# A recurrent layer with a feed-forward gate: order of the first projections, of z and of the odd products

## The chip, the cores and the metric

The kernel runs on one core of a Trainium2 chip. The metric is the device time of one execution in microseconds (us), as the median of several runs. The engines are called PE (TensorE, matrix products), DVE (VectorE), ACT (ScalarE), POOL (GpSimd) and SP (SyncE); each works through its own queue of instructions, and SP and POOL also issue the DMA transfers here.

## The reference

All in float32, S = 2048 tokens, hidden width 512, H = 16 heads of D = 128, four lags:

```python
xn = layernorm(x)                                    # 2048 x 512
q, k, v = (conv4(silu(xn @ W)) for W in (Wq, Wk, Wv))  # causal, 4 taps per channel, 2048 x 2048
z, a, b = xn @ Wz, xn @ Wa, xn @ Wb                  # a, b: 16 wide
q, k = rotary(q), rotary(k)                          # then each head divided by its norm
out = 0
for s in range(4):                                   # lag s: s tokens earlier
    attn = einsum('bshd,bshd->bsh', q, lag(k, s)) / sqrt(D)
    out += (attn * sigmoid(lag(a, s) * b))[..., None] * lag(v, s)
out = out * rsqrt(mean(out * out) + eps) * norm_w * silu(z)
s = out @ Wout                                       # 2048 x 512
hidden = relu((xn @ sign(up).T) * up_scale)          # 2048 x 2048
g = silu((hidden @ sign(down).T) * down_scale * out_scale)
return x + s * g
```

## The kernel before

**Tiling.** Features lie on the 128 partitions and tokens along the free axis. The tokens are cut into NTB = 4 blocks of TB = 512 (index b), the 16 heads into NP = 8 pairs (index p); a pair has two halves j of 128 channels. `xnT` holds the normalised input feature-major. One projection of a pair (pq, pk, pv or pz) is 8 matmuls of 128x512 with K = 4 chunks, each seen as two rows of the profile, so sixteen rows.

**A step.** `step(p, b)` first makes `queries(p, b + 1)` and `products(p, b + 1)`: pq, silu, a convolution by one ACT multiply and three DVE operations for each half; pk in the same way; the rotation by lags (`turn`); and the products of q and k for four lags, tile `pr`, first for half 0 and then for half 1. For blocks after the first and odd p, half 1 goes through the tile `half` in two parts (L367 to L370); for even p it fills a second `pr` tile and a POOL DMA adds it. The sums over channels (`dots`) are made by PE from pairs of p. Then, for block b itself: pv, the convolution of v (`values`), the output projections that are due (`output_projections`, with `sum_dots` in the middle), the load of the z weights, the load of `wo`, pz (`gates_of_output`), the weighted sum over lags (`weighted`: `o` from `v` and the coefficients `bc`, seven DVE operations), and `gated_output` (`oz`: two DVE operations). After an odd p, the output projection of the pair p - 1, p is put on a list; it is worked off in the next step. So the projection of pairs 0 and 1 is done in step p = 2, and that of 2 and 3 in step p = 4. The gated output of p = 0 is held back until step p = 1 (`first_due`).

**Around the blocks.** A first pass of steps with b = -1 makes the q and k side of block 0, with the feed-forward part of block 0 between. Three passes follow, and then the last block has a loop of its own (L756), which only has v, z and the output side. The coefficients of a block are written to DRAM (`co_dram`) and loaded again as `bc`, spread over the partitions. At the end come the feed-forward products of blocks 1 to 3 and the gate of the outputs.

**What sets the order.** What goes through the class `InOrder` (`pe`, `dve`, `pool`, and `loads["by"]` in the last block) stays in the program's order on its engine; all of it shows as L76 in the profile. What is issued by `nc.scalar`, `nc.sync` and `nc.gpsimd` directly is placed by a scheduler within the dependencies. The tile q has one buffer, `pr` two, the weights' tile `w` three, the PSUM pool `mm` six banks.

**The start.** Four chunks of x are loaded, measured, normalised (`first_layer_norm`) and transposed on PE (`transpose`), each followed by an idle matmul that keeps PE busy (`idle_work`). Only then comes the first pq.

Of the kernel before, what the change touches and what calls it, by code (L numbers as in the profile page):

```python
# [44 lines left out]
P = 128  # L45
# [4 lines left out]
LAGS = 4  # L50
# [31 lines left out]
def recurrent_layer(ctx: ExitStack, tc: tile.TileContext, a: dict, out: bass.AP):  # L82
    nc = tc.nc
    pe, dve = InOrder(tc, nc.tensor), InOrder(tc, nc.vector)

    pool = InOrder(tc, nc.gpsimd)
    loads = {"by": nc.sync}

    const = ctx.enter_context(tc.tile_pool(name="const", bufs=1))
# [42 lines left out]
    nc.gpsimd.memset(no_ab, 0.0)  # L132

    def small_loads():
        nc.sync.dma_start(conv_w, a["conv_w"])
        nc.sync.dma_start(w_ab, a["w_ab"])
        nc.sync.dma_start(ab_dram[:, 0:HALO], no_ab)
        nc.sync.dma_start(turns, a["turns"])
        nc.sync.dma_start(of_head, a["of_head"])
        nc.sync.dma_start(of_heads, a["of_heads"])  # L140
        nc.sync.dma_start(norm_w, a["norm_w"])
        nc.sync.dma_start(up_scale, a["up_scale"])
# [3 lines left out]

    def first_layer_norm():

        mv = qks.tile([P, TC, 2], F32, tag="mv", name="mv0", bufs=2)
        rstd = qks.tile([P, TC], F32, tag="rstd", name="rstd0", bufs=2)  # L150
        x_in = qks.tile([P, TC, HID], F32, tag="pr", name="x_in0", bufs=2)

        def normalise(c):
            one = slice(c, c + 1)
            nc.scalar.activation(rstd[:, one], mv[:, one, 1], AF.Sqrt, bias=eps_ln)
            dve.reciprocal(rstd[:, one], rstd[:, one])
            dve.tensor_scalar(
                x_in[:, c, :], x_in[:, c, :], mv[:, c, 0:1], rstd[:, one], ALU.subtract, ALU.mult
            )

        for c in range(TC):
            nc.sync.dma_start(x_in[:, c, :], a["x"][c * P : (c + 1) * P, :])
            st = qks.tile([P, 6], F32, tag="st", name=f"st{c}", bufs=2)
            dve.bn_stats(st, x_in[:, c, :])
            dve.bn_aggr(mv[:, c, :], st)
            if c:
                normalise(c - 1)
        normalise(TC - 1)
        return x_in

    def transpose(x_in, idle_work):
        for c in range(TC):
            tp = mm.tile([P, KC, P], F32, tag="mm", name=f"tp{c}")
            for k in range(KC):
                pe.transpose(tp[:, k, :], x_in[:, c, k * P : (k + 1) * P], ident)
            idle_work(TB // 2)
            nc.scalar.copy(xnT[:, :, HALO + c * P : HALO + (c + 1) * P], tp)  # L177

    means = {}

    def statistics(b, c):
# [79 lines left out]
    def keep_halo(name, t, p, b):  # L261
        if b < NTB - 1:
            nc.scalar.copy(kept[name][:, p], t[:, :, TB : TB + HALO])

    def project(n, p, b, to):
        for j in range(2):
            pp = mm.tile([P, TB], F32, tag="mm", name=f"p{n}{j}_{p}_{b}")
            for k in range(KC):
                pe.matmul(
                    pp,  # L270
                    weights[n][:, k, j * P : (j + 1) * P],
                    xnT[:, k, HALO + b * TB : HALO + (b + 1) * TB],
                    start=(k == 0),
                    stop=(k == KC - 1),
                )
            nc.scalar.activation(to[:, j, :], pp, AF.Silu)
# [27 lines left out]

    def queries(p, b):

        load(qks, "q", p, b)
        q = qks.tile([P, LAGS, 2, TB], F32, tag="q", name=f"q_{p}_{b}", bufs=1)
        q0 = q[:, LAGS - 1]
        convolve(0, p, raw_of(qks, "q", p, b), q0)  # L310
        return q
# [16 lines left out]
    def products(p, b, q, between=None, beside_k=None):  # L328

        n = f"_{p}_{b}"  # L330
        load(qks, "k", p, b)
        q0 = q[:, LAGS - 1]
        k = with_halo(qks, "k", "k", 1, p, b)
        raw = raw_of(qks, "k", p, b)
# [24 lines left out]
        if not b or p % 2 == 0:  # L359
            pr1 = qks.tile([P, LAGS, TB], F32, tag="pr", name="pr1" + n, bufs=2)  # L360
            product(pr1, 1, 0, LAGS)
            if b:
                nc.gpsimd.dma_start(pr, pr1, accum_op=ALU.add)
            elif p < NP - 1:
                dve.tensor_tensor(pr, pr, pr1, ALU.add)
        else:
            for lo in range(0, LAGS, 2):  # L367
                half = qks.tile([P, 2, TB], F32, tag="half", name=f"half{lo}" + n, bufs=1)
                product(half, 1, lo, lo + 2)
                dve.tensor_tensor(pr[:, lo : lo + 2], pr[:, lo : lo + 2], half, ALU.add)  # L370
        if not b:

            prs = [pr, pr1] if p == NP - 1 else [pr]
# [191 lines left out]
    def step(p, b, beside_q=None, beside_k=None):  # L565

        at = b >= 0
        change = p == 0 and at
        q = queries(p, b + 1)
        if beside_q:  # L570
            beside_q()
        if change and b:
            sum_squares()
            norms(b)
        due = bool(dots_due) and dots_due[0][-1]
        if change and not b:

            def beside_k():
                norms(b)
                norms_in_rows(b)  # L580

        products(p, b + 1, q, (lambda: norms_in_rows(b)) if change and b else None, beside_k)
        if p == NP - 1 and b + 2 < NTB:
            gate_products(b + 2)
        if at:
            load(vs, "v", p, b)
            raw = raw_of(vs, "v", p, b, 1)
        if first_due:
            first_due.pop()()
        if at:  # L590
            v = values(p, b, raw)

        output_projections(sum_dots if due else None)
        if change:
            coefficients(b)
        if at:
            load(vs, "z", p, b)
            wo = load_wo(p, b)
            z = gates_of_output(p, b)
            out_of = lambda: gated_output(p, b, weighted(p, b, v), z, wo)  # L600
            if change:
                first_due.append(out_of)
            else:
                out_of()
        if p == 1 and at:
            gate(b + 1)
        if b + 2 < NTB:
            if p < TC:
                statistics(b + 2, p)
            if p == TC - 1:  # L610
                centre(b + 2)
            elif p == 5:
                divide(b + 2)
# [8 lines left out]

    for n in (TB, TB, TB // 2):
        idle_work(n)
    x_in = first_layer_norm()
    small_loads()
    transpose(x_in, idle_work)
    def in_two_terms(pool, x, tag, bufs, shape, name):
        hi = pool.tile(shape, F32R, tag=f"{tag}_hi", name=f"{name}_hi", bufs=bufs)
        lo = pool.tile(shape, F32R, tag=f"{tag}_lo", name=f"{name}_lo", bufs=bufs)  # L630
# [23 lines left out]
    with tc.tile_pool(name="pre", bufs=1, side="right") as pre:  # L654
        signs = {}

        def fetch(g, which):

            for f in range(G * g, G * g + G):
                raw = pre.tile([P, HID], F32, tag="raw", name=f"pre_{which}_raw{f}", bufs=4)  # L660
                src = a[which][f]
                nc.sync.dma_start(raw, src.rearrange("p k m -> p (k m)") if which == "up" else src)
                sign = pre.tile([P, HID], F32R, tag="sign", name=f"pre_{which}{f}", bufs=8)
                nc.scalar.activation(sign, raw, AF.Sign)
                nc.gpsimd.dma_start(signs_dram[which][:, f], sign)
                signs[which, f] = sign

# [25 lines left out]
                else:  # L693
                    nc.gpsimd.dma_start(to, part, accum_op=ALU.add)

        xs = in_two_terms(pre, tokens(0), "xs", 1, [P, KC, TB], "xs0")
        for p in range(NP):
            g = p // 2
            if p == 0:

                def first_ups():
                    fetch(0, "up")
                    ups(0, G)

                step(p, -1, None, first_ups)
            elif p % 2 == 0:
                step(p, -1, lambda: ups(G * g, G * g + 2), lambda: ups(G * g + 2, G * g + G))
            else:
# [22 lines left out]
    raw = raw_of(vs, "v", 1, last, 1)  # L731
    load(vs, "v", 2, last)
    wo = load_wo(0, last)
    sum_dots()
    coefficients(last)
    output_projections()
# [19 lines left out]
    for p in range(NP + 1):  # L756
        if 1 < p < NP:
            weights["v"] = v_weights.pop(p)
            raw = raw_of(vs, "v", p, last, 1)
        if p:  # L760
            z = gates_of_output(p - 1, last)
        if p % 2 == 1:
            output_projections()
        if 0 < p < NP:
            load(vs, "z", p, last)
            v = values(p, last, raw)
        if p and p + 2 < NP:
            load(vs, "v", p + 2, last)
# [27 lines left out]
    with tc.tile_pool(name="ff", bufs=1, side="right") as ff, tc.tile_pool(  # L796
# [6 lines left out]
        def ends(b, banks=None):  # L803
# [17 lines left out]
                    g, banks[c] if banks else g, out_scale, down_scale, ALU.mult, ALU.mult  # L821
                )

            def gate(c):
                rows, x, y, g = loaded[c]
                t = b * TC + c
                nc.scalar.activation(g, g, AF.Silu)
                dve.scalar_tensor_tensor(g, y, rms[:, t : t + 1], g, ALU.mult, ALU.mult)
                dve.tensor_tensor(g, g, x, ALU.add)
                nc.sync.dma_start(out[rows, :], g)  # L830

            return scale, gate

        def down_projection(c, f, terms):
# [10 lines left out]
        for b in range(1, NTB):  # L845
            pf = [pfs.tile([P, HID], F32, name=f"pf{c}") for c in range(TC)]
            for f in range(2, NFC + 2):
# [22 lines left out]
            scale, gate = ends(b, pf)  # L870
            if b == last:

                for cs in (0, 1), (2,), (3,):
                    for _, df, terms in hids:
                        for c in cs:
                            down_projection(c, df, terms)
                    for c in cs:
                        scale(c)
                        if c:
                            gate(c - 1)  # L880
                gate(TC - 1)
            else:

                for c in range(TC):
                    scale(c)

# [69 lines left out]
```

## Time and profile before

| what | value |
|---|---|
| median of 3 runs | 1429.37 us (1429.17 to 1430.85) |
| the profiled execution | 1430.83 us, its span 1429.0 us |
| mean granted clock of PE | 0.995 |
| busy: PE, DVE, ACT, POOL | 1405.1, 1209.7, 612.0, 231.3 us |
| chain that ended last | PE 63%, DVE 22%, issue 6%, DMA 3%, ACT 3% |

A group's row gives line, engine and operation, output and inputs, count, then busy time and mean ns of one, then the idle time of the engine ahead of it and what ended most of it. A row of the timeline gives start and duration in us, engine, line, operation, output and inputs, count, and in brackets the idle time before it with what ended that.

### The profile page before, as it was taken

What the parts mean: (1) busy time and instruction counts of PE and PEld (TensorE: products, weight loads), DVE (VectorE), ACT (ScalarE), POOL (GpSimd) and SP (SyncE); (2) the same over time, 40 slices, a digit from 0 to 9 for tenths busy, and PEclk for the clock granted to TensorE, in tenths of its full rate; (3) what the DMA queues carried; (4) which work ended last, traced back from release to release, by engine and by line L of the source; (5) the groups of instructions that cost most, each with busy time, mean ns of one, the idle gap of its engine ahead of it and who ended that gap; (6) DMA issues with size and microseconds to landing.
All of it is one profiled execution on the core that took longest, in us unless ns stands there. A gap on an engine that the chain in (4) does not pass through costs nothing.

```text
span 1429.0 us, 12596 instructions
## 1 busy us (share of the span) xinstructions
PE 1405.1 (98%) x3958; PEld 686.0 (48%) x3958; DVE 1209.7 (85%) x1363; ACT 612.0 (43%) x1181; POOL 231.3 (16%) x317
## 2 busy tenths in 40 slices
PE   9999999899999999999999999999999999999998
PEld 5555544344444444444444444444443444578886
DVE  6999988999999979999999899999995979146454
ACT  7475545445444443444434444444342323232122
POOL 2222121111212220112122201121211111200000
PEclk9999999999999999999999999999999999999999
DMA  9879676987998688779986897796848888662030
GB/s 327 252 195 206 154 200 133 250 194 190 188 226 194 135 176 234 201 166 196 220 205 147 168 236 192 177 206 174 165 88 211 238 208 203 125 235 90 30 89 30
DMA packets 101779, 259.22 MB, mean 181 GB/s; under 512 B 18833, under 2 KB 19345, under 8 KB 97361
## 3 DMA queue, kind: packets, MB, share of 16 engines
q0 software_dynamic: 33088, 104.89, 38.8%
q1 hardware_dynamic: 68624, 153.53, 35.4%
q8 instruction: 32, 0.52, 0.2%
q14 instruction: 35, 0.28, 0.1%
HBM read 157.67 MB, written 35.68 MB: 135 GB/s over the span
## 4 chain that ended last, share of the span: by engine, by line
PE 63%; DVE 22%; issue 6%; DMA 3%; ACT 3%; SPq 1%; POOL 0%; DVEq 0%; POOLq 0%; ACTq 0%
PE po L76 13%; PE pz L76 11%; PE pv L76 9%; PE pq L76 8%; PE pk L76 8%; PE pf L76 6%; PE ph L76 6%; DVE q L76 5%; DVE pr L76 3%; DVE k L76 3%; DVE o L76 3%; DVE te L76 2%; DVE v L76 2%; DVE half L76 1%; PE dots L76 1%
## 5 line engine op out<-in xcount | busy, mean ns | idle before, releaser
L76 PE MATMUL po<-wo,oz 128*128 128x512 f32 x512 | 228.8, 601 | 10.0 <-DVE oz L76 10.0
L76 PE MATMUL pz<-xnT,wz 128*128 128x512 f32 x512 | 227.2, 596 | 3.2 <-DMA wz<-in_wz_dram 3.2
L76 PE MATMUL pv<-xnT,wv 128*128 128x512 f32 x512 | 226.4, 594 | 0.0
L76 PE MATMUL pq<-xnT,wq 128*128 128x512 f32 x512 | 226.0, 593 | 0.2 <-ACT xnT L177 0.2
L76 PE MATMUL pk<-xnT,wk 128*128 128x512 f32 x512 | 225.2, 592 | 0.0
L76 PEld LDWEIGHTS po<-wo,oz 128*128 128x128 f32 x512 | 97.0, 192 | 139.1 <-issue 112.5
L76 DVE SCALAR_TENSOR_TENSOR k<-rk,conv_w,k 128x512 f32<-128x512 f32 x192 | 142.0, 751 | 25.4 <-ACT k L288 20.8
L76 DVE SCALAR_TENSOR_TENSOR q<-rq,conv_w,q 128x512 f32<-128x512 f32 x192 | 141.3, 749 | 22.1 <-ACT q L288 17.5
L76 PEld LDWEIGHTS pz<-xnT,wz 128*128 128x128 f32 x512 | 97.0, 190 | 129.1 <-issue 125.5
L76 PEld LDWEIGHTS pv<-xnT,wv 128*128 128x128 f32 x512 | 95.7, 189 | 127.7 <-issue 117.2
L76 PEld LDWEIGHTS pq<-xnT,wq 128*128 128x128 f32 x512 | 96.0, 189 | 126.1 <-issue 118.0
L76 PEld LDWEIGHTS pk<-xnT,wk 128*128 128x128 f32 x512 | 96.6, 189 | 121.0 <-issue 117.1
L76 DVE SCALAR_TENSOR_TENSOR v<-rv,conv_w,v 128x512 f32<-128x512 f32 x192 | 141.3, 750 | 4.8 <-ACT v L288 0.3
L76 DVE SCALAR_TENSOR_TENSOR q<-q,turns 128x1024 f32<-128x1024 f32 (+1 forms) x128 | 127.1, 1013 | 2.3
L76 DVE TENSOR_TENSOR o<-o,te 128x1024 f32<-128x1024 f32 x96 | 117.5, 1224 | 3.3
L76 DVE TENSOR_TENSOR pr<-q,k 128x2048 f32<-128x2048 f32 x52 | 117.3, 2286 | 0.9
L76 DVE TENSOR_TENSOR te<-v,bc 128x1024 f32<-128x1024 f32 x96 | 116.9, 1218 | 1.0 <-DMA bc<-co_dram 1.0
L649 ACT ACTIVATE hid<-ph,up_scale 128x512 f32<-128x512 f32 x64 | 43.8, 685 | 119.4 <-PE ph L76 118.8
L76 DVE CAST hid_hi<-hid 128x512 fp32r<-128x512 f32 x64 | 27.1, 423 | 71.9 <-ACT hid L649 71.9
L76 PE MATMUL ph<-xs_hi,up 128*128 128x512 f32 x192 | 76.4, 398 | 0.7 <-ACT so_sb L423 0.7
L76 PE MATMUL ph<-xs_lo,up 128*128 128x512 f32 x192 | 75.8, 395 | 0.0
L547 ACT COPY part<-po 128x512 f32<-128x512 f32 x64 | 37.1, 580 | 84.8 <-PE po L76 49.5
(142 smaller groups left out, 1662.6 us busy)
## 6 DMA issues: line engine op xcount, KB each, us to landing
bc<-co_dram SPq DMA_DIRECT2D x128, 256.0 KB, 6.4
pr<-pr POOLq DMA_DIRECT2D x72, 256.0 KB, 5.6
wq<-in_wq_dram SPq DMA_DIRECT2D x32, 512.0 KB, 6.5
wk<-in_wk_dram SPq DMA_DIRECT2D x32, 512.0 KB, 5.8
sq<-sq POOLq DMA_DIRECT2D x32, 512.0 KB, 5.7
wv<-in_wv_dram SPq DMA_DIRECT2D x32, 512.0 KB, 6.6
wz<-in_wz_dram SPq DMA_DIRECT2D x32, 512.0 KB, 6.0
wo<-in_wo_dram SPq DMA_DIRECT2D x32, 512.0 KB, 6.4
```

Source lines behind the costliest of these rows:

```text
L76: return self.tc.keep_in_program_order(getattr(self.engine, op)(*args, **kwargs))
L547: nc.scalar.copy(part, po)
L649: nc.scalar.activation(hid, ph, AF.Relu, scale=up_scale[:, f : f + 1])
```

## The change

Five edits:

- At the start, statistics and normalising go by halves of the four chunks, ACT keeps the program's order there (`act`), the loads of the first q and k weights go ahead of the small loads, and the first pq is computed by halves of the tokens (`first_product`): the first 256 tokens of both j after two chunks are transposed. Chunks 2 and 3 are transposed within it, and two idle matmuls are gone.
- In step p = 2 of each block, pz goes ahead of the output projections.
- For odd p after the first block, the product of half 1 is written into q's place (`q[:, :, 1]`) and then added to `pr`: for p = 1 by a POOL DMA of 1 MB, for the others by one DVE operation.
- In the last block the z weights of pairs 1 and on are requested one step sooner, those of pair 1 ahead of the coefficients.
- The last down projections of the feed-forward part go in another order of chunks, and the last operations of the ends are written out in one order.

```diff
+    act = InOrder(tc, nc.scalar)
...
     def small_loads():
-        nc.sync.dma_start(conv_w, a["conv_w"])
...
-        for c in range(TC):
-            nc.sync.dma_start(x_in[:, c, :], a["x"][c * P : (c + 1) * P, :])
...
-            if c:
-                normalise(c - 1)
-        normalise(TC - 1)
-        return x_in
...
+        for c in range(TC):
+            nc.sync.dma_start(x_in[:, c, :], a["x"][c * P : (c + 1) * P, :])
+        for half in range(2):
+            for c in range(2 * half, 2 * half + 2):
+                measure(c)
+            for c in range(2 * half, 2 * half + 2):
+                normalise(c)
+        transpose(0)
+        idle_work(TB // 2)
+        transpose(1)
+        idle_work(TB // 2)
+
+        return lambda: (transpose(2), transpose(3))
...
+    def first_product(to, second_half):
+
+        pps = [mm.tile([P, TB], F32, tag="mm", name=f"pq{j}_0_0") for j in range(2)]
+        for lo in range(0, TB, TB // 2):
+            for j in range(2):
+                for k in range(KC):
+                    pe.matmul(
+                        pps[j][:, lo : lo + TB // 2],
+                        weights["q"][:, k, j * P : (j + 1) * P],
+                        xnT[:, k, HALO + lo : HALO + lo + TB // 2],
+                        start=(k == 0),
+                        stop=(k == KC - 1),
+                    )
+                if lo == j == 0:
+                    second_half()
+        for j in range(2):
+            act.activation(to[:, j, :], pps[j], AF.Silu)
...
         else:
-            for lo in range(0, LAGS, 2):
-                half = qks.tile([P, 2, TB], F32, tag="half", name=f"half{lo}" + n, bufs=1)
-                product(half, 1, lo, lo + 2)
-                dve.tensor_tensor(pr[:, lo : lo + 2], pr[:, lo : lo + 2], half, ALU.add)
+
+            product(q[:, :, 1], 1, 0, LAGS)
+            if p == 1:
+
+                nc.gpsimd.dma_start(pr, q[:, :, 1], accum_op=ALU.add)
+            else:
+                dve.tensor_tensor(pr, pr, q[:, :, 1], ALU.add)
...
-        output_projections(sum_dots if due else None)
+        midway = sum_dots if due else None
+
+        late = at and p == 2
+        if not late:
+            output_projections(midway)
         if change:
             coefficients(b)
         if at:
             load(vs, "z", p, b)
             wo = load_wo(p, b)
             z = gates_of_output(p, b)
+            if late:
+                output_projections(midway)
...
-    x_in = first_layer_norm()
+    other_chunks = first_layer_norm()
+    load(qks, "q", 0, 0)
+    nc.sync.dma_start(conv_w, a["conv_w"])
+    load(qks, "k", 0, 0)
     small_loads()
-    transpose(x_in, idle_work)
...
     wo = load_wo(0, last)
+    z_weights = {0: weights["z"]}
+    load(vs, "z", 1, last)
+    z_weights[1] = weights["z"]
     sum_dots()
     coefficients(last)
...
         if p:
+            weights["z"] = z_weights.pop(p - 1)
             z = gates_of_output(p - 1, last)
         if p % 2 == 1:
             output_projections()
+        if 1 < p < NP:
+            load(vs, "z", p, last)
+            z_weights[p] = weights["z"]
         if 0 < p < NP:
-            load(vs, "z", p, last)
             v = values(p, last, raw)
...
-                for cs in (0, 1), (2,), (3,):
-                    for _, df, terms in hids:
-                        for c in cs:
-                            down_projection(c, df, terms)
-                    for c in cs:
-                        scale(c)
-                        if c:
-                            gate(c - 1)
-                gate(TC - 1)
+                downs(0, 0, n - 1)
+                downs(1, 0, 2)
+                downs(0, n - 1, n)
+                downs(1, 2, n)
+                by_y(0)
+                plus_x(0)
+                by_y(1)
+                downs(2, 0, n)
+                plus_x(1)
+                by_y(2)
+                downs(3, 0, n)
+                plus_x(2)
+                by_y(3)
+                plus_x(3)
```

Here `downs(c, lo, hi)` makes the products of chunk c with the hidden chunks lo to hi and, after the last of them, the chunk's scale and silu; `by_y` multiplies by the attention's output, `plus_x` adds x and stores the chunk.

More of the change, by code (lines that the diff above doesn't have):

```diff
@@ L151, in first_layer_norm, with measure @@
         x_in = qks.tile([P, TC, HID], F32, tag="pr", name="x_in0", bufs=2)
+        def measure(c):
+            st = qks.tile([P, 6], F32, tag="st", name=f"st{c}", bufs=2)
+            dve.bn_stats(st, x_in[:, c, :])
+            dve.bn_aggr(mv[:, c, :], st)
+            one = slice(c, c + 1)
+            act.activation(rstd[:, one], mv[:, one, 1], AF.Sqrt, bias=eps_ln)
         def normalise(c):
             one = slice(c, c + 1)
-            nc.scalar.activation(rstd[:, one], mv[:, one, 1], AF.Sqrt, bias=eps_ln)
             dve.reciprocal(rstd[:, one], rstd[:, one])
@@ L159, in normalise, with transpose @@
             )
-        for c in range(TC):
-            nc.sync.dma_start(x_in[:, c, :], a["x"][c * P : (c + 1) * P, :])
-            st = qks.tile([P, 6], F32, tag="st", name=f"st{c}", bufs=2)
-            dve.bn_stats(st, x_in[:, c, :])
-            dve.bn_aggr(mv[:, c, :], st)
-            if c:
-                normalise(c - 1)
-        normalise(TC - 1)
-        return x_in
-    def transpose(x_in, idle_work):
-        for c in range(TC):
+        def transpose(c):
             tp = mm.tile([P, KC, P], F32, tag="mm", name=f"tp{c}")
@@ L175, in transpose @@
                 pe.transpose(tp[:, k, :], x_in[:, c, k * P : (k + 1) * P], ident)
-            idle_work(TB // 2)
-            nc.scalar.copy(xnT[:, :, HALO + c * P : HALO + (c + 1) * P], tp)
+            act.copy(xnT[:, :, HALO + c * P : HALO + (c + 1) * P], tp)
+        for c in range(TC):
[10 more added lines that the diff above has]
+        return lambda: (transpose(2), transpose(3))
+    means = {}
     means = {}
@@ L263, in keep_halo @@
             nc.scalar.copy(kept[name][:, p], t[:, :, TB : TB + HALO])
+    def first_product(to, second_half):
[14 more added lines that the diff above has]
+            act.activation(to[:, j, :], pps[j], AF.Silu)
     def project(n, p, b, to):
+        if n == "q" and p == b == 0:
+            first_product(to, second_half)
+            return
         for j in range(2):
@@ L305, in queries @@
     def queries(p, b):
-        load(qks, "q", p, b)
+        if p or b:
+            load(qks, "q", p, b)
         q = qks.tile([P, LAGS, 2, TB], F32, tag="q", name=f"q_{p}_{b}", bufs=1)
@@ L330, in products @@
         n = f"_{p}_{b}"
-        load(qks, "k", p, b)
+        if p or b:
+            load(qks, "k", p, b)
         q0 = q[:, LAGS - 1]
@@ L663, in fetch @@
                 sign = pre.tile([P, HID], F32R, tag="sign", name=f"pre_{which}{f}", bufs=8)
-                nc.scalar.activation(sign, raw, AF.Sign)
+                (act if f < G else nc.scalar).activation(sign, raw, AF.Sign)
                 nc.gpsimd.dma_start(signs_dram[which][:, f], sign)
@@ L694, in downs, with second_half @@
                     nc.gpsimd.dma_start(to, part, accum_op=ALU.add)
-        xs = in_two_terms(pre, tokens(0), "xs", 1, [P, KC, TB], "xs0")
+        xs = None
+        def second_half():
+            nonlocal xs
+            other_chunks()
+            xs = in_two_terms(pre, tokens(0), "xs", 1, [P, KC, TB], "xs0")
         for p in range(NP):
@@ L699, in recurrent_layer @@
             if p == 0:
[L701 to L705, printed above, removed]
+                step(p, -1, lambda: fetch(0, "up"), lambda: ups(0, G))
             elif p % 2 == 0:
@@ L822, in scale, with silu, by_y, plus_x @@
                 )
-            def gate(c):
-                rows, x, y, g = loaded[c]
+            def silu(c):
+                g = loaded[c][-1]
+                nc.scalar.activation(g, g, AF.Silu)
+            def by_y(c):
+                _, _, y, g = loaded[c]
                 t = b * TC + c
-                nc.scalar.activation(g, g, AF.Silu)
                 dve.scalar_tensor_tensor(g, y, rms[:, t : t + 1], g, ALU.mult, ALU.mult)
+            def plus_x(c):
+                rows, x, _, g = loaded[c]
                 dve.tensor_tensor(g, g, x, ALU.add)
                 nc.sync.dma_start(out[rows, :], g)
+            def gate(c):
+                silu(c)
+                by_y(c)
+                plus_x(c)
+            if b == last:
+                return scale, silu, by_y, plus_x
             return scale, gate
@@ L869, in recurrent_layer, with downs @@
                     down_projection(c, df, terms)
-            scale, gate = ends(b, pf)
             if b == last:
-                for cs in (0, 1), (2,), (3,):
-                    for _, df, terms in hids:
-                        for c in cs:
-                            down_projection(c, df, terms)
-                    for c in cs:
-                        scale(c)
-                        if c:
-                            gate(c - 1)
-                gate(TC - 1)
+                scale, silu, by_y, plus_x = ends(b, pf)
+                n = len(hids)
+                def downs(c, lo, hi):
+                    for _, df, terms in hids[lo:hi]:
+                        down_projection(c, df, terms)
+                    if hi == n:
+                        scale(c)
+                        silu(c)
+                downs(0, 0, n - 1)
[12 more added lines that the diff above has]
+                plus_x(3)
             else:
+                scale, gate = ends(b, pf)
                 for c in range(TC):
```

## Prediction

> **What bounds the kernel now.** I read the page's engine shares first, then the groups of TensorE (PE) with the idle time ahead of them, then the timeline around each idle stretch.
>
> ```profile
> PE 1405.1 (98%) x3958; PEld 686.0 (48%) x3958; DVE 1209.7 (85%) x1363; ACT 612.0 (43%) x1181; POOL 231.3 (16%) x317
> L76 PE MATMUL po<-wo,oz 128*128 128x512 f32 x512 | 228.8, 601 | 10.0 <-DVE oz L76 10.0
> L76 PE MATMUL pz<-xnT,wz 128*128 128x512 f32 x512 | 227.2, 596 | 3.2 <-DMA wz<-in_wz_dram 3.2
> ```
>
> PE is busy for 98% of the span, and no matmul is added or removed but two idle ones. So the time can come only from PE's idle stretches and from what a lowered clock costs after them. Two waits hold 13.2 us: output projections for VectorE's (DVE's) gated output `oz`, and z projections for their weights. The timeline of PE places them:
>
> ```profile
> 274.95 1.88 PE L76 MATMUL po<-wo,oz 128*128 128x512 f32 x4
> 283.58 8.08 PE L76 MATMUL po<-wo,oz 128*128 128x512 f32 x12 [6.75 <-DVE oz L76]
> 575.01 5.42 PE L76 MATMUL po<-wo,oz 128*128 128x512 f32 x12 [1.86 <-DVE oz L76]
> 863.31 5.42 PE L76 MATMUL po<-wo,oz 128*128 128x512 f32 x12 [1.39 <-DVE oz L76]
> 1101.21 8.80 PE L76 MATMUL pz<-xnT,wz 128*128 128x512 f32 x16 [3.18 <-DMA wz<-in_wz_dram]
> ```
>
> In each of the first three blocks the first output projection begins with four rows on the even pair's `oz` and then waits for the odd pair's. The wait of 6.75 us costs more than itself: the twelve rows behind it took 8.08 us where the same twelve took 5.42 at 575.01, and the granted clock is half from 282.16 to 288.98. After the 3.18 us at 1101.21 sixteen rows took 8.80 where sixteen take 6.87 elsewhere (1109.85 to 1116.72), half clock again. After 1.86 and 1.39 us nothing was lost.
>
> Next, how full DVE is around the first stall and up to the next output projection (busy time of PE, PE's weight loads, DVE, ACT and POOL, then clock, DMA share and GB/s):
>
> ```profile
> 225.00:283.60 58.60, 51.85 (x127) 22.04 (x126) 57.32 (x59) 25.18 (x55) 5.92 (x8) 0.99 0.82 207
> 283.60:356.00 72.40, 72.40 (x173) 30.93 (x174) 68.32 (x77) 34.10 (x67) 11.78 (x16) 0.96 0.79 192
> ```
>
> DVE works 57.3 of 58.6 us and then 68.3 of 72.4, with rows following each other up to the next `oz`. PE is late because DVE is. So PE gets back only what DVE can follow.
>
> **Part 2, z ahead of the first output projection (p = 2).** From the first po row at 274.95 to the next block's pq at 306.43 are 31.48 us. The work in it is 6.87 (pz) + 4 x 3.43 (po) + 1.0 (dots) = 21.6. With pz first, PE reaches the odd `oz` at 274.95 + 6.87 + 1.72 = 283.54, and DVE has its first half ready near 283.5 even if it gains nothing: the stall and its half clock go, 9.85 us. The z weights were issued at 263.58 and land in about 8 us, before 274.95. The later stalls give 1.86 and 1.39.
>
> What is late next is `oz` of p = 3:
>
> ```profile
> 351.44 1.41 DVE L76 SCALAR_TENSOR_TENSOR oz<-o,norm_w,z 128x512 f32<-128x512 f32 x2
> ...
> 355.70 7.03 PE L76 MATMUL po<-wo,oz 128*128 128x512 f32 x16
> ```
>
> Its first half is ready at about 352.2; PE needs it after four po rows, 357.42. The slack is 5.2 us, PE comes 9.85 earlier, and DVE earlier by part 3 only.
>
> **Part 3, odd products in q's place.** Four operations of 1.22 us (the two `half` products and their adds, 4.91 with gaps) become one product of 2.29 and, for p = 3, 5, 7, an add of the same shape (two such rows take 4.46): DVE saves 0.45. For p = 1 a GpSimd DMA adds 1 MB, and DVE saves 2.6. But that DMA reads q, so ScalarE's (ACT's) next q convolution, which began right after the old product, now waits for its landing, and ACT works its queue in order:
>
> ```profile
> 256.18 1.22 DVE L76 TENSOR_TENSOR pr<-pr,half 128x1024 f32<-128x1024 f32 x1
> 259.42 0.72 ACT L288 ACTIVATE q<-rq,conv_w 128x512 f32<-128x512 f32 x1
> 267.12 1.33 ACT L288 ACTIVATE v<-rv,conv_w 128x512 f32<-128x512 f32 x2
> 269.61 4.57 DVE L76 SCALAR_TENSOR_TENSOR v<-rv,conv_w,v 128x512 f32<-128x512 f32 x6
> ```
>
> Queued behind that wait on ACT are the second q eviction, both v multiplies at 267.12 that DVE's v convolution needs, the z and k evictions. The twelve 1 MB adds in this trace took 8.2 to 15.6 us from issue to landing (9.0 in the middle). The new product ends at about 257.15, so the DMA issues at 257.45 and, at 9.6 us (load here is 0.82 of the DMA engines, above the middle), lands at 267.0. The v convolution then starts about 1.45 us later, at 268.5 rather than 269.61: DVE gains 1.0 us there, not 2.6. Each us of a later landing is lost again one for one. On POOL the four small adds for the pair's dots follow the landing: they were ready at 274.3, now some 7 us later, and PE needs them near 289. That cover holds.
>
> So `oz` of p = 3 is ready at 352.2 - 1.0 - 0.45 = 350.75, PE asks at 357.42 - 9.85 = 347.57, and a new stall of 3.2 us stands there. It may lower the clock as the 3.18 us did (up to 1.7): I add 0.7. Block 0 gives 9.85 - 3.2 - 0.7 = 6.0, between 4.5 and 6.7. Later pairs of the block have slacks of 6.2 and 7.8 before, so nothing is lost behind it. In the next blocks the slacks at p = 3 are 2.6 and 4.2, more than the 1.86 and 1.39 gained, so these are kept.
>
> [...]
>
> **Part 5, z weights of the last block sooner.** They were issued at 1092.49, behind loads of `bc` that waited for the coefficients' write until 1089.84. Requested earlier, the 3.18 us and the slow sixteen rows (8.80 against 6.87) go: 5.1 us. But the next PE step that needs DVE has little slack:
>
> ```profile
> 1095.42 1.23 DVE L76 TENSOR_TENSOR o<-v,bc 128x1024 f32<-128x1024 f32 x1 [10.60 <-DMA bc<-co_dram]
> ...
> 1123.61 1.41 DVE L76 SCALAR_TENSOR_TENSOR oz<-o,norm_w,z 128x512 f32<-128x512 f32 x2
> ```
>
> This `oz` is half ready at 1124.35, and PE, on po from 1123.59, needs it at 1125.31: slack 1.0. DVE's chain starts with the landing of `bc`, which the change does not hasten, and runs on almost without idle time. So 4.1 of the 5.1 come back as a wait at that po, longer than the 3.18 that lowered the clock (up to 1.9 more; I take 0.9), and the weights' 512 KB now share the DMA engines with the coefficients and `bc` (0 to 1.7 later; I take 0.6). Net: 5.1 - 4.1 - 0.9 - 0.6 = -0.5, between -2.6 and +1.0.
>
> **Part 1, the start.** The wq load goes ahead of the small ones, and the first pq runs by halves of the tokens, the first half ahead of chunks 2 and 3. But ACT still takes all four Sqrts (the last at 8.23) ahead of its first copy at 8.6, so pq can start near 9.8, not 11.08; two transposes (0.95) then lie inside it, and 32 half rows take a little more than 16 whole ones. PE reaches pk at 17.7 to 18.3 instead of 18.05, and now idles about 2 us ahead of pq, which may cost clock (up to 1.7). I take -0.2, between -2.0 and +0.6.
>
> **The tail.** In the order after, the third chunk's add (0.69) no longer stands between the last scale and the last two operations: +0.65.
>
> **Sum.** -0.2 + 6.0 + 1.86 + 1.39 - 0.5 + 0.65 = 9.2 us. The profiled execution took 1430.83 (span 1429.0 and 1.83 around it), so it would take 1421.6; it lay 1.46 above the median of 1429.37, so the same gain on the median gives **1420.2**.
>
> **The rivals.** *DVE keeps up:* all stalls go without successors, 9.85 + 1.86 + 1.39 + 5.1 + 0.65 = 18.9, or 1410.5. For it: 85% mean load on DVE. Against: the two windows and the chain from 1095.42, which have no idle time to give. Chance 0.10.
>
> *ACT behind the 1 MB add:* in three blocks the q convolution's wait takes the place of the stall removed. Each us of landing beyond 9.6 costs block 0 one us, block 1 one beyond its slack of 2.6, block 2 one beyond 4.2. At 15 us that is 5.4 + 2.8 + 1.2 = 9.4, the whole gain: from there on the kernel is slower. At 18 us it is 8.4 + 5.8 + 4.2 = 18.4, and the time 1438.6. For it: 15.6 us did occur. Against: it occurred once in twelve, beside a load that is not at p = 1. Chance 0.10.
>
> *Given back:* the new stalls at p = 3, in the last block and at the start each lower the clock and the DMA lands 2 us later: block 0 gives 3.0, the last block -2.6, the start -2.0, and 1.86 + 1.39 + 0.65 stay: 2.3 us, 1427.1. Milder mixtures reach to 1424.5. Chance 0.20, of which about half lies within 0.2%.
>
> **How the numbers follow.** 0.2% (2.9 us) is about what a measurement of this kernel can tell from no change. My forecast's own range, 1416 to 1424.5, has 0.60. Faster by over 0.2%: 0.60 + 0.10 + 0.11 = 0.81; within: 0.09; slower: 0.10. For 8 in 10 the range runs from 1413 to 1427, which leaves out most of the two outer rivals.
>
> **What would show it.** Right: no wait of po for `oz` at p = 1 of the first three blocks, and a new one of about 3 us at p = 3 of the first; q's convolution on ACT waiting for the DMA of `pr` at p = 1; no wait of pz for wz near 1100, and about 4 us at the po behind it; pk starting near 18. Wrong: DVE idle time ahead of `oz` of p = 3, landings of the 1 MB adds of 13 us and more, or a half clock in places where PE had no gap of 3 us.

## The result, and the profile after

The changed kernel took 1440.97 us in the median of ten runs (1431.3 to 1448.97), the kernel before 1429.88 in ten (1426.27 to 1432.46). The ratio is 1.0076, with a 95% interval of 1.0053 to 1.0100: slower by about 11 us, where 9.2 us of gain were forecast. The profiled execution was the shortest of the ten (1431.3, span 1429.5), so it shows the mechanisms but not the usual size of the loss. The first experiment below profiles the same kernel again at 1442.96 (span 1441.1).

First the groups of PE and DVE with their waits, on the page of the profiled execution after:

```profile
L76 PE MATMUL po<-wo,oz 128*128 128x512 f32 x512 | 229.3, 602 | 9.0 <-DVE oz L76 9.0
L76 PE MATMUL pk<-xnT,wk 128*128 128x512 f32 x512 | 225.3, 592 | 2.4 <-DMA wk<-in_wk_dram 2.4
L76 PE MATMUL pz<-xnT,wz 128*128 128x512 f32 x512 | 225.4, 592 | 0.0
L76 DVE SCALAR_TENSOR_TENSOR v<-rv,conv_w,v 128x512 f32<-128x512 f32 x192 | 141.3, 750 | 16.9 <-ACT v L319 12.4
L319 ACT ACTIVATE q<-rq,conv_w 128x512 f32<-128x512 f32 x64 | 45.2, 718 | 49.8 <-DMA pr<-q 26.0
```

The wait of pz for its weights is gone; pk waits 2.4 us for its own, once, in block 2 (849.00). The wait of po for `oz` is 9.0 us instead of 10.0: it has moved. DVE's v convolution, which lost 0.3 us to ACT before, now loses 12.4. Its row on the page before:

```profile
L76 DVE SCALAR_TENSOR_TENSOR v<-rv,conv_w,v 128x512 f32<-128x512 f32 x192 | 141.3, 750 | 4.8 <-ACT v L288 0.3
```

ACT's q convolution has a wait that did not exist, 26.0 us for the add by DMA. The timeline of PE places the waits of po:

```profile
284.24 7.03 PE L76 MATMUL po<-wo,oz 128*128 128x512 f32 x16
...
353.96 8.39 PE L76 MATMUL po<-wo,oz 128*128 128x512 f32 x12 [3.41 <-DVE oz L76]
647.45 5.42 PE L76 MATMUL po<-wo,oz 128*128 128x512 f32 x12 [2.55 <-DVE oz L76]
1126.43 12.28 PE L76 MATMUL po<-wo,oz 128*128 128x512 f32 x28 [3.02 <-DVE oz L76]
```

The first output projection of block 0 runs through without a wait, as forecast. The new waits stand at p = 3 of block 0 (3.41, forecast 3.2), at p = 3 of block 1 (none was forecast) and behind the z weights of the last block (3.02, forecast 4.1).

The same kernel profiled at 1442.96, timeline of PE:

```profile
646.37 7.11 PE L76 MATMUL po<-wo,oz 128*128 128x512 f32 x12 [3.69 <-DVE oz L76]
...
938.18 5.42 PE L76 MATMUL po<-wo,oz 128*128 128x512 f32 x12 [2.12 <-DVE oz L76]
...
1076.00 1.94 PE L76 MATMUL dots<-pr,of_heads 128*32 128x512 f32 x8 [4.00 <-DMA pr<-pr]
1077.87 15.69 PE L76 MATMUL po<-wo,oz 128*128 128x512 f32 x32
...
1136.47 13.68 PE L76 MATMUL po<-wo,oz 128*128 128x512 f32 x28 [5.33 <-DVE oz L76]
```

The waits in block 1 and in the last block are longer, there is one more in block 2 (938.18), and at the change to the last block PE waits 4.00 us for the last products' small DMA adds and then runs at half clock (8 dots in 1.94 us, where 1.06 is usual; 32 rows of po in 15.69, where 14.00 is usual).

How far each profile's PE is behind (+) or ahead (-) of the kernel before, in us, at the start of the same work (times of the kernel before in the first row):

| | first pk of block 0's pass, 201.8 | pk of p=3, 313.3 | pk of p=5, 384.4 | block 1, p=3, 602.1 | p=5, 673.1 | block 2, p=5, 961.4 | last block, 1083.1 | 1144.2 | end of span |
|---|---|---|---|---|---|---|---|---|---|
| after, 1431.3 | +2.3 | -7.0 | -0.4 | -1.4 | +1.4 | +2.3 | +3.1 | +1.2 | +0.5 |
| after, 1442.96 | +3.0 | -6.1 | -1.7 | -3.7 | +2.0 | +3.8 | +10.4 | +12.7 | +12.1 |
| DVE add at p=1 | +2.5 | -7.2 | -2.1 | -4.2 | -4.2 | -5.9 | -5.9 | -2.8 | -3.8 |
| best version | -0.4 | -9.9 | -5.5 | -7.6 | -7.6 | -9.2 | -8.5 | -11.6 | -12.5 |

The two last rows are experiments told below.

### The profile page after: what moved, and what is told of

The parts are those of the page before. It is cut to its first block, busy times and chain, and to the rows that moved or that the text cites. A ratio compares the mean times of both kernels' runs of the same rounds, so it can differ in the third digit from the quotient of the medians.

```text
span 1429.5 us, 12606 instructions
## 1 busy us (share of the span) xinstructions
PE 1404.3 (98%) x3970; PEld 687.8 (48%) x3970; DVE 1199.7 (84%) x1336; ACT 601.5 (42%) x1181; POOL 235.2 (16%) x320
## 5 line engine op out<-in xcount | busy, mean ns | idle before, releaser
L76 PE MATMUL pq<-xnT,wq 128*128 128x512 f32 (+1 forms) x528 | 226.2, 581 | 1.7 <-ACT xnT L76 1.7
L76 PEld LDWEIGHTS pq<-xnT,wq 128*128 128x128 f32 x528 | 99.0, 189 | 124.9 <-issue 114.1
L76 DVE SCALAR_TENSOR_TENSOR v<-rv,conv_w,v 128x512 f32<-128x512 f32 x192 | 141.3, 750 | 16.9 <-ACT v L319 12.4
L319 ACT ACTIVATE q<-rq,conv_w 128x512 f32<-128x512 f32 x64 | 45.2, 718 | 49.8 <-DMA pr<-q 26.0
```

What stands on the lines that cost most here:

```text
L76: return self.tc.keep_in_program_order(getattr(self.engine, op)(*args, **kwargs))
L319: nc.scalar.mul(to[:, j, :], raw[:, j, HALO:], conv_w[:, i, p, j, LAGS - 1 : LAGS])
```

## The experiments

Each experiment's ratio is to the kernel before measured beside it, whose median lay between 1430.1 and 1432.1 us; the ratios compare better than the times. Three theories were put up. START: the reordered start makes the first pass late. ADD: the 1 MB add by DMA at p = 1 holds up ACT. STALLS: the new waits for `oz` with their half clock make the loss.

**The changed kernel again** (no edit).

> The changed kernel once more, for a profile of one of its usual executions (ten took 1431.3 to 1449.0, and the profiled one was the shortest). Its time should be near 1441. Theory START (the reordered start makes the signs of the feed-forward weights late, and PE waits in the first pass): PE has idle time and half clock before 200 us, and the first pz comes 8 to 12 us later than the 218.7 of the kernel before. Theory ADD (the 1 MB add by DMA at p = 1 holds up ACT): the first pz is within 3 us of 218.7, and ACT waits over 10 us for the add in each of three blocks, with PE idle behind it. Theory STALLS (new waits for oz at p = 3 and in the last block, each with half clock): neither, but 3 to 5 us of idle and 3 us of half clock at each of four places.

Measured 1442.96 (ratio 1.0083, 1.0068 to 1.0098). The first pass is 3 us late, so START makes at most that. In the three passes the add landed 9.5, 15.0 and 16.5 us after its issue. The third one, on ACT, DVE and POOL (three timelines of this profile, from p = 1 of block 2):

```profile
843.86 0.60 ACT L307 ACTIVATE rq<-pq 128x512 f32<-128x512 f32 x1 [4.73 <-PE pq L76]
856.05 0.72 ACT L319 ACTIVATE q<-rq,conv_w 128x512 f32<-128x512 f32 x1 [11.59 <-DMA pr<-q]
...
856.77 1.33 ACT L319 ACTIVATE v<-rv,conv_w 128x512 f32<-128x512 f32 x2
```

```profile
847.26 1.42 DVE L76 SCALAR_TENSOR_TENSOR oz<-o,norm_w,z 128x512 f32<-128x512 f32 x2
857.52 4.57 DVE L76 SCALAR_TENSOR_TENSOR v<-rv,conv_w,v 128x512 f32<-128x512 f32 x6 [8.85 <-ACT v L319]
```

```profile
839.49 1.31 POOL L404 DMA_DIRECT2D pr<-q  x1 [7.05 <-issue]
856.56 1.06 POOL L420 DMA_DIRECT2D pr<-pr  x2 [15.76 <-DMA pr<-q]
```

ACT has the q of the next pair ready to convolve at 844.5 and waits 11.59 us for the landing; DVE has finished `oz` at 848.7 and stands 8.85 us until ACT, right behind, has multiplied v. In block 1 it stands 7.40 us, in block 0 1.87. ADD predicted waits over 10 us in each pass and PE idle behind them; ACT's waits are 9.45, 10.62 and 11.59, and PE waits for `oz` in each of these blocks.

**The start as before, all else changed.**

```diff
-    act = InOrder(tc, nc.scalar)
...
-    other_chunks = first_layer_norm()
-    load(qks, "q", 0, 0)
-    nc.sync.dma_start(conv_w, a["conv_w"])
-    load(qks, "k", 0, 0)
+    x_in = first_layer_norm()
     small_loads()
+    transpose(x_in, idle_work)
```

> The changed kernel with the start as it was before; all other edits stay. START: about 1428 to 1431, 10 us below the changed kernel or more, and the spread falls to 3 us. ADD and STALLS: within 2 us of the changed kernel (1439 to 1443).

Measured 1439.84 (1.0057, 1.0036 to 1.0079): START is not the main cause.

**The add at p = 1 by DVE.**

```diff
-            if p == 1:
-                nc.gpsimd.dma_start(pr, q[:, :, 1], accum_op=ALU.add)
-            else:
-                dve.tensor_tensor(pr, pr, q[:, :, 1], ALU.add)
+            dve.tensor_tensor(pr, pr, q[:, :, 1], ALU.add)
```

> The changed kernel with the add at p = 1 made by DVE as at p = 3, 5, 7 (no 1 MB DMA). ADD: 8 to 12 us faster than the changed kernel, about 1431, less spread. START: the same within 2 us. DVE has 2.3 us more to do in three blocks, so in the first block the oz of p = 3 would be about 1 us later than in the profiled execution if the DMA cost nothing.

Measured 1429.02 (0.9987, 0.9975 to 0.9999). The one edit takes back 13 to 14 us (1.0076 and 1.0083 against 0.9987), and with it the waits at p = 3 of blocks 1 and 2 and at the dots are gone. So these stalls are an effect of the add, and STALLS is not a theory beside it; the waits at p = 3 of block 0 (3.18) and in the last block (5.33) stay. The table shows where the loss arises: up to the start of p = 3 of block 1 this variant and the repeat differ by at most 1.1 us.

**The start alone**, on the kernel before: statistics and normalising by halves, the loads' order, `act`, and the first product by halves of tokens.

```diff
+        if n == "q" and p == b == 0:
+            first_product(to, second_half)
+            return
...
-                step(p, -1, None, first_ups)
+                step(p, -1, lambda: fetch(0, "up"), lambda: ups(0, G))
```

> The kernel before with only the reordered start. START: 1436 to 1442, all of the loss and its spread. ADD and STALLS: 1428 to 1431, as the kernel before (pk 0.5 us sooner).

Measured 1432.73 (1.0016, 1.0004 to 1.0027): 2 us of loss, neither of the two expectations. The loss is small but real; the experiment on the signs looks for its place.

**The product of p = 1 in a tile of its own, still added by DMA.** This separates ACT's wait from the transfer. (The tile takes 8 KB per partition, for which `te` gives up its second buffer.)

```diff
-            product(q[:, :, 1], 1, 0, LAGS)
+            second = q[:, :, 1]
+            if p == 1:
+                second = qks.tile([P, LAGS, TB], F32, tag="half", name="half" + n, bufs=1)
+            product(second, 1, 0, LAGS)
             if p == 1:
-                nc.gpsimd.dma_start(pr, q[:, :, 1], accum_op=ALU.add)
+                nc.gpsimd.dma_start(pr, second, accum_op=ALU.add)
...
-                te = vs.tile([P, 2, TB], F32, tag="te", name=f"te{s}" + n, bufs=2)
+                te = vs.tile([P, 2, TB], F32, tag="te", name=f"te{s}" + n, bufs=1)
```

> The changed kernel with the product of p = 1 in a tile of its own: the 1 MB add by DMA stays, but ACT's next q convolution no longer waits for it. WAIT (the loss is ACT standing behind the add's landing): about the time of the variant with the DVE add (1429.0) or up to 4 us below, since DVE has 2.3 us less to do in three blocks. TRAFFIC (the loss is the megabyte itself, on the DMA engines and on POOL's queue, which delays coefficients, weights and the pair's sums): 1438 to 1443, as the changed kernel.

Measured 1425.28 (0.9958, 0.9942 to 0.9975): WAIT, and not TRAFFIC. POOL, ACT and DVE of this profile at p = 1 of block 1 (three timelines):

```profile
546.97 0.86 POOL L406 DMA_DIRECT2D pr<-half  x1 [7.11 <-issue]
560.32 1.05 POOL L422 DMA_DIRECT2D pr<-pr  x2 [12.48 <-DMA pr<-half]
```

```profile
550.89 0.60 ACT L307 ACTIVATE rq<-pq 128x512 f32<-128x512 f32 x1 [4.26 <-PE pq L76]
551.52 0.72 ACT L319 ACTIVATE q<-rq,conv_w 128x512 f32<-128x512 f32 x1
```

```profile
555.00 1.42 DVE L76 SCALAR_TENSOR_TENSOR oz<-o,norm_w,z 128x512 f32<-128x512 f32 x2
556.34 4.56 DVE L76 SCALAR_TENSOR_TENSOR v<-rv,conv_w,v 128x512 f32<-128x512 f32 x6
```

The megabyte still takes some 13 us, but ACT's q convolution starts at once and DVE goes from `oz` to v without idle time. The landing is also 2 to 3 us shorter than in the repeat, but that does not explain it: in the changed kernel a landing of 12.8 us would still have cost DVE some 5 us (see "What a landing costs" below). In this profile nobody stands behind the transfer, and it is cheap: 0.9958 with it, 0.9987 with DVE's add.

**DVE add and the start as before.** Both edits shown above together.

> DVE add at p = 1 and the start as before; z ahead, the sooner z weights and the tail stay. START costs 2.3 us by the first pz of the profiles (220.96 against 218.71): 1426.5 with the theory that this stays to the end; 1429 if a later wait swallows it.

Measured 1426.14 (0.9959, 0.9942 to 0.9975), against 0.9987 (0.9975 to 0.9999) with the reordered start: the start's loss stays to the end.

**The same without the sooner z weights.**

```diff
-    z_weights = {0: weights["z"]}
-    load(vs, "z", 1, last)
-    z_weights[1] = weights["z"]
...
-        if 1 < p < NP:
-            load(vs, "z", p, last)
-            z_weights[p] = weights["z"]
         if 0 < p < NP:
+            load(vs, "z", p, last)
             v = values(p, last, raw)
```

> As the one before, and the last block's z weights requested where they were. In the profile of the variant with the DVE add PE waited 5.33 us for oz behind the z weights and then took 14.72 for 28 rows (12.0 at full clock), while the wait removed and its half clock were worth 5.1. Theory GIVEN BACK: 1423 to 1426, 0 to 3 us better than with the sooner request. Theory that the sooner request gains: 1429 to 1431.

Measured 1422.16 (0.9930, 0.9917 to 0.9943), 4 us better than with them. GIVEN BACK is too mild: the sooner request costs.

**The sooner z weights alone**, on the kernel before.

```diff
     wo = load_wo(0, last)
+    z_weights = {0: weights["z"]}
+    load(vs, "z", 1, last)
+    z_weights[1] = weights["z"]
     sum_dots()
     coefficients(last)
```

> The kernel before with only the sooner z weights of the last block. The prediction put 0.5 us of loss on it (2.6 of loss to 1.0 of gain): 1429.5 to 1433 where the kernel before is at 1431. From the two variants with DVE adds it costs 4 us: 1434 to 1436.

Measured 1435.05 (1.0032, 1.0020 to 1.0044), 4.6 us of loss. SP, DVE and PE of this profile (three timelines):

```profile
1084.43 0.38 SPq L76 DMA_DIRECT2D wz<-in_wz_dram  x1
1087.33 0.33 SPq L464 DMA_DIRECT2D co_dram<-rk  x1
1094.59 2.60 SPq L76 DMA_DIRECT2D bc<-co_dram  x4
```

```profile
1100.77 1.23 DVE L76 TENSOR_TENSOR o<-v,bc 128x1024 f32<-128x1024 f32 x1 [13.46 <-DMA bc<-co_dram]
```

```profile
1130.33 13.78 PE L76 MATMUL po<-wo,oz 128*128 128x512 f32 x28 [5.33 <-DVE oz L76]
```

In the kernel before, SP issues the coefficients' write and the `bc` loads so:

```profile
1084.85 0.33 SPq L464 DMA_DIRECT2D co_dram<-rk  x1
1089.84 2.61 SPq L76 DMA_DIRECT2D bc<-co_dram  x4
```

The weights, requested 2.9 us ahead of the coefficients' write, lengthen it: from its issue until the `bc` loads start it takes 7.26 us, 4.99 before. In the eight profiles with the sooner request this takes 5.3 to 7.3 us, in the six without 2.7 to 5.0. DVE starts on `bc` 13.4 us after that issue, 10.6 before. The 2.9 us go straight to the po that had a slack of 1.0, and behind its wait PE runs at half clock (28 rows 13.78, 12.28 at full clock). This profile's span is 6.4 us longer than that of the kernel before, but 2.7 of these were lost ahead of the last block, where the edit changes nothing.

**z ahead alone**, on the kernel before.

```diff
-        output_projections(sum_dots if due else None)
+        midway = sum_dots if due else None
+        late = at and p == 2
+        if not late:
+            output_projections(midway)
...
             z = gates_of_output(p, b)
+            if late:
+                output_projections(midway)
```

> The kernel before with pz ahead of the first output projection and nothing else. By the prediction's working: 9.85 + 1.86 + 1.39 given, and a new wait at p = 3 of the first block of 9.85 - 5.2 = 4.6 us, with about 3 us of half clock behind it as in the changed kernel's profile: 5 to 6 us faster, 1425. If DVE is late in the other blocks too: 1428 to 1430.

Measured 1424.80 (0.9951, 0.9935 to 0.9966): 7 us better, 1 to 2 more than expected. In the profile PE is 9.0 us further ahead at p = 3 of block 0 than at the block's start, gives 7.0 back by p = 5 (4.16 us of wait, and half clock behind it: 12 rows 8.01, 5.42 in the kernel before), and gains 2.1 and 1.7 in the next two blocks.

**The add by DMA in the first pass only.**

```diff
-            if p == 1:
+            if p == 1 and b == 1:
```

> The changed kernel with the add by DMA in the first pass only, where it landed after 9.6 us in all three profiles; DVE adds it in the next two passes, where it landed after 11.6 to 16.5. Theory WAIT with the price of one us for each us of landing: near the variant with DVE adds throughout, 1429, within 2 us. A theory in which every such add costs alike, 4.6 us each: 1433 to 1435.

Measured 1427.97 (0.9983, 0.9970 to 0.9996), as with DVE adds throughout (0.9987). The one add landed after 9.6 us. There it costs no more than DVE's own add; the loss comes from the second and third.

**The signs freed, start alone.**

```diff
-                (act if f < G else nc.scalar).activation(sign, raw, AF.Sign)
+                nc.scalar.activation(sign, raw, AF.Sign)
```

> The reordered start alone, but with the signs of the first four up weights not held in ACT's program order behind the first silu. If these late signs make the start's loss of 2 us (the four buffers of raw weights come free 6 us later, and the next loads with them): 1430 to 1431, the kernel before or 0.5 us less. If the loss comes from the two idle us of PE ahead of pq or from the later split of the inputs: 1432.5 to 1433.5, as with the start alone.

Measured 1432.48 (1.0016, 1.0006 to 1.0026): no better, so the late signs are not it. The profile shows PE waiting for DVE's hidden terms in the first pass, where the kernel before had two waits of 0.2 us:

```profile
133.97 0.50 PE L76 MATMUL pf<-pre_down,hid_hi 128*128 128x512 f32 x1 [1.39 <-DVE hid_hi L76]
```

DVE began this cast 1.45 us later than before (133.50 against 132.05), while PE came 0.2 us earlier. The same wait stands in the profiles of the start alone (1.41) and of the repeat (1.42). Behind it, in the start alone, the seven rows of pf from 136.75 to 139.31 begin every 0.43 us, where the three from 132.01 to 132.47 begin every 0.23: half clock. What set DVE back is not settled: with the reordered start it splits xnT 2.2 us later (13.27 against 11.06), but that it is this alone was not tried.

**All that gained, together:** z ahead, the tile of its own with the DMA add, DVE adds at p = 3, 5, 7, the tail; start and z weights as before. The edits are those shown above, put together.

> z ahead, the product of p = 1 in a tile of its own with the add by DMA, DVE adds for p = 3, 5, 7, and the tail; the start and the last block's z weights as before. With WAIT as the cause, this has all the gains seen so far and none of the losses: the variant without start and sooner z weights was at 0.9930 of the kernel before, and the tile of its own took 0.3% off the DVE add: 0.990 to 0.992, 1417 to 1419. If the 1 MB transfers cost as much as DVE saves: 0.993.

Measured 1418.39 against 1430.12 (0.9923, 0.9908 to 0.9939): 11 us faster than the kernel before, and by their two ratios 1.5% faster than the changed kernel. From the page of this profile:

```profile
L76 PE MATMUL po<-wo,oz 128*128 128x512 f32 x512 | 227.9, 599 | 4.4 <-DVE oz L76 4.4
```

That the tile of its own beats the DVE add in this setting isn't shown: the intervals (0.9908 to 0.9939 and 0.9917 to 0.9943) overlap.

## Why the prediction was wrong

**The step that failed is the landing of the add in part 3.** The mechanism was named, with ACT's queue and what stands in it, and block 0 fits: the landing was put at 9.6 us and came after 9.6, 9.5 and 9.6 in the profiles of the changed kernel, of its repeat and of the one with the old start. The failure was to let block 0 stand for all three. In blocks 1 and 2 the add landed after 13.8 and 11.6 us in the profiled execution of 1431.3, after 15.0 and 16.5 in the repeat, after 15.0 and 16.0 with the old start. The prediction read the load of the DMA engines from one window, 0.82 in 225 to 283.6 (the stretch of the add in block 0 has 0.70), and gave blocks 1 and 2 no landing of their own. Had it asked the trace of the kernel before for the stretches of the three adds, it would have seen this (columns as in the prediction's windows; the last two are DMA share and GB/s):

```profile
257.45:267.05 9.60, 9.60 (x27) 4.03 (x29) 9.46 (x9) 2.87 (x7) 2.28 (x4) 1.00 0.70 173
545.00:560.00 15.00, 15.00 (x36) 6.61 (x35) 14.76 (x13) 4.52 (x10) 2.61 (x4) 1.00 0.99 291
835.00:851.50 16.50, 16.50 (x39) 7.18 (x38) 16.19 (x16) 7.27 (x13) 2.62 (x4) 1.00 0.98 286
```

In block 0 the DMA engines move 173 GB/s, in blocks 1 and 2 they are full (0.99 and 0.98) at 291 and 286, without the add. In the repeated run, beside the add's 1.05 MB, the queue of plain transfers moved 0.56 MB while it was under way in block 0, 3.19 in block 1 and 3.52 in block 2, mainly weights and `bc`. So longer landings were to be expected there. The twelve adds of the kernel before point the same way: the one of 15.6 us (issued at 379.20) had 2.35 MB of plain transfers beside it, one of 8.2 us (882.27) 0.41. The prediction set the 15.6 aside as a load that p = 1 does not meet, but the windows above hold 3.50 MB in block 1 and 3.87 in block 2. That just 15 to 16.5 us could have been read from this is not shown.

**What a landing costs.** In the profiles of the changed kernel, of its repeat and of the one with the old start, DVE's wait ahead of v is the landing less 7.6 us in all nine cases: 1.96, 6.17 and 3.99 us in the first, 1.87, 7.40 and 8.85 in the repeat, 1.97, 7.37 and 8.36 with the old start. For so long DVE is busy with the weighted sum and `oz` anyway. So the prediction's "lost again one for one" was right for DVE. In the repeat the three waits sum to 18.1 us, and the adds had saved DVE 3 x 2.3 = 6.9; the 11.2 left are most of what the DVE add took back. In the execution of 1431.3 only 12.1 - 6.9 = 5.2 are left, and its span is 4.4 us above that of the profile with the DVE add. That fits the small loss of this execution; that the landings make the whole spread of 1431 to 1449 is not shown.

**The price was too low as well.** The rival "ACT behind the 1 MB add" had the right mechanism, and its break-even of 15 us was close to the landings that came. But for 15.0 and 16.5 us its formula gives (15.0 - 9.6 - 2.6) + (16.5 - 9.6 - 4.2) = 5.5 us; the DVE add took back 13 to 14. The formula took the slacks at p = 3 from the kernel before, though PE comes earlier now (3.7 us ahead at p = 3 of block 1 in the repeat), and let them end the matter. In the table the repeat loses 5.7 us against the DVE add at p = 3 of block 1, 3.5 more up to p = 5 of block 2, and then 6.6 more at the change to the last block: there the products of p = 7 were late, their chain of small adds landed 4.00 us after PE asked, and half clock followed (8 dots 1.94, 1.06 usual). DVE did not make up its delay: the `oz` that starts at 862.50 in the kernel before comes 8.2 us later in the repeat, and the first product of p = 7 (1048.48) 9.8 us later. A slack taken at one point does not say what is left at the others.

**What held, and what else was mis-sized.** z ahead: 9.85 forecast for block 0; 9.3 in the profile after (from +2.3 to -7.0). The new wait at p = 3: 3.2 forecast, 3.41 measured, 2.44 in the repeat. Half clock behind it: 0.7 allowed, 3.0 measured (12 rows 8.39 against 5.42, the granted clock half from 353.15 to 359.97) and 1.7 in the repeat (7.11), so block 0 gave 2.7 and 4.7 net instead of 6.0. In blocks 1 and 2 the removed waits came back about as forecast (1.86 and 1.39) where no late add was in the way (2.1 and 1.7 in z ahead alone). Part 5 was mis-sized: -0.5 forecast, 4.6 us of loss measured alone, since DVE's start on `bc` came 2.9 us later (0.6 taken) and the half clock cost 1.5 (0.9 taken). Part 1: -0.2 forecast, about 2 us of loss measured alone (1.0016); pk did start sooner (17.58), but the count ended at pk, and the price fell due at 134 us, where DVE was late; why it was late stays open. The tail: 0.65 forecast; between the last up projections and the end the profiles show 0.2 to 0.4.

**"DVE keeps up"** is ruled out: PE waits for `oz` at p = 3 of block 0 even with z ahead alone (4.16 us), and the best version still has 4.4 us of such waits. Of the prediction's signs of being wrong two came: landings of 13 us and more, and half clock behind a gap under 3 us (2.44 in the repeat).

## What to carry to other kernels

A transfer that takes a job off a busy engine must be priced at every place where it runs, with the DMA load of that place (in the repeat the same megabyte landed after 9.5 us in block 0 and after 16.5 in block 2), and by who is queued behind its landing. Writing its source into a buffer that the next step needs at once turned a cheap background transfer into waits of ACT's queue, of up to 11.59 us in the repeat; a buffer of its own made the kernel with the same transfer 17 us faster (1.0076 against 0.9958). And look what is under way when a load is requested sooner, and whether that is the transfer on the critical chain: with the z weights requested 2.9 us ahead of it, the coefficients' write took 7.26 us here instead of 4.99.

## What the runs showed of the hardware

In these runs half clock did not follow from the length of a wait alone. Two timelines of PE, first of the kernel with the sooner z weights alone, then of z ahead with DVE adds:

```profile
575.98 7.11 PE L76 MATMUL po<-wo,oz 128*128 128x512 f32 x12 [1.86 <-DVE oz L76]
```

```profile
352.46 5.42 PE L76 MATMUL po<-wo,oz 128*128 128x512 f32 x12 [3.77 <-DVE oz L76]
```

1.86 us of idle cost 1.7 us in the first; 3.77 cost nothing in the second. The kernel before has a wait of 1.86 us at the same place (575.01), and there the twelve rows took 5.42. After 1.88 us (the tile of its own, p = 3 of block 0) and 2.44 (the repeat, p = 3 of block 0) they took 7.11, after 2.55 (the profiled execution of 1431.3, p = 3 of block 1) and 2.12 (the repeat, p = 3 of block 2) 5.42. The granted clock is half for 6.83 us from 282.15 and for 3.41 from 1101.35 in the kernel before, and for 6.83 from 353.15 in the changed one. What decides besides the length of the wait is not shown. The prediction's line at gaps of 3 us did not hold: waits of 1.86, 1.88 and 2.44 us cost 1.7, and one of 3.77 nothing.
